# A third turn of lead for an image's parts, built at image 33 instead of 11, with another sharing-out of the weights' steps

## The chip, the core and the metric

The kernel runs on one NeuronCore of a Trainium2 chip. The metric is the device time of one execution in microseconds (us). The engines are named as in the profile: PE is TensorE, DVE is VectorE, ACT is ScalarE, POOL is GpSimd, SP is the queue that starts most DMAs.

## The reference

```python
# x: (160, 128, 32, 32) f32; U: 5 sets of 128*128*9 weights
s1 = (max(U) - min(U)) / 3;  v1 = s1 * floor(U / s1)
s2 = s1 / 5;                 v2 = s2 * floor((U - v1) / s2)
w = v1 + v2                       # the quantised weights of 5 grouped 3x3 convolutions
z = groupnorm(x, 32 groups of 4 channels, eps=1e-5)
out = x + conv3x3(z, w)           # images 0..31 by the first set, 32..63 by the second, ...
```

The sets are spread over the batch as channel groups; in the kernel's own order, set n serves the 32 images from 32n on. Each image is 128 channels (partitions) of 1024 values.

## The kernel before, in words

The whole program is one stream of 160 images on one core, written out in Python with a fixed order on each engine. In the loop of `run`, one pass is the **turn** of image `i`. In it, PE first does `sums_of_pairs(i + 1)` and then the main matmuls of image `i` (`conv`, `main`). The other engines work for images ahead of `i` and for the one behind.

Every image is split into a high and a low fp16 part, so that fp16 matmuls give the precision of fp32. There are two ways of doing an image:

- A **combined** image adds and subtracts neighbouring columns before the split. DVE and POOL make `v` (`combine`, L690 and L697 on DVE; `outer_columns` L678 and the subtraction at L708 on POOL), ACT makes the high part `vh` (L738), and DVE the low part `vl` (L744). Its PE work is 24 matmuls.
- An **uncombined** image has `z` (L714 on POOL, or L640 on ACT for the first of a group), `hi` (L648 on ACT), and on DVE `lo` (L751) and its row combinations (L764, L772, L773). Its PE work is 30 matmuls.

Up to image 29 the odd images from 7 on are combined; from 30 to 129 those with `i % 5` of 0, 2 or 4; later three in four.

The steps of an image `k` come in this order on DVE, in different turns:

1. `combine(k)`, if `k` is combined, at the end of the turn that `step_of(i, 4)` gives it;
2. after ACT's high part in the next turn (`step_of(i, 3)`), `vl` or `lo` with its combinations in the turn after that (`step_of(i, 2)`);
3. in turn `k - 1`, `pairs(k)`: two DVE instructions (L903, L905), which put halves of the sums that PE left in PSUM into the two banks in which `main(k)` accumulates. PE's `main(k)` waits for them; they wait for `sums_of_pairs(k)` on PE and for the copy `leave(k)` on ACT (L891).

The distance from these steps to the image's own turn is set by `step_of`:

```python
change = self.FURTHER + 4 - ahead
return [k for k in range(i + ahead + (i > change), i + ahead + 1 + (i >= change)) if k < self.imgs]
```

Until the turn `change` the step is for image `i + ahead`, after it for `i + ahead + 1`, and in that turn for both. With FURTHER = 11, two images are combined in turn 11, get their high parts in turn 12 and their low parts in turn 13. From then on low parts are ready three turns before their `main` instead of two. `consumed` uses the same constant: it tells from which turn on a chunk of two input images may be overwritten by a new load on SP.

DVE also measures eight early images itself (`BY_VECTOR`: 8, 10, 11, 14, 19, 24, 29, 34; L231 to L235); ACT measures the others. Further small DVE work belongs to the statistics of a group of images (L296 to L302, L307, L310), and POOL takes the power of the variance (L286).

While set n is in use, set n+1 is quantised. The weights' work is a list of DVE steps (L142 to L146, L162, L549, then L573 to L575), with two steps per column for ACT between them. The object `later` hands them out: each turn adds `pace` to what is due (36 / 22 for the first such set, 36 / 25 for the others), and `later.take(1)` issues one step if one is due and the next one isn't ACT's. There are up to three places in a turn: after L751 of an uncombined image, after the low part, and after `combine`.

The instruction `before` decides when POOL begins its share (L286, L678, L708, L714) for the image four turns ahead: these instructions wait for it, so that they run beside `pairs`[...].

```python
last = later.take(1, last)
if last:
    before = self.last_but_one(last)
```

Of the kernel before, what the change touches and what calls it, by code (L numbers as in the profile page):

```python
# [36 lines left out]
class Later:  # L37
# [25 lines left out]
    def finish(self):  # L63
        run(self.steps)
# [110 lines left out]
def last_of(steps, last=None):  # L175
    for last in steps:
        pass
    return last


def run(steps):

    while True:
        try:
            next(steps)
        except StopIteration as end:
            return end.value
# [134 lines left out]
def general_path(tc, keep, steps, x, u, out):  # L322
# [8 lines left out]
    with tc.If(far > 0), ExitStack() as ctx:  # L331
# [9 lines left out]
        for n in range(N_SETS):  # L341
            un = one.tile([P, C, TAPS], F32, tag="u", name=f"g_u{n}")
            nc.sync.dma_start(un, uv[n])
            wn = one.tile([P, C, TAPS], F32, tag="w", name=f"g_w{n}")
            k1, k2 = run(steps.quantise(one, un, f"g{n}", F32))
            nc.vector.tensor_scalar_mul(wn, k1, steps.s1)
            nc.vector.scalar_tensor_tensor(wn, k2, steps.s2, wn, ALU.mult, ALU.add)
# [38 lines left out]
class Main:  # L386
# [22 lines left out]


    STAT_LEAD = 15
    FURTHER = 11
    LOAD_LEAD = 18
    CHUNKS = 11
    STEADY = 7
# [557 lines left out]
    def step_of(self, i, ahead):  # L973


        change = self.FURTHER + 4 - ahead
        return [k for k in range(i + ahead + (i > change), i + ahead + 1 + (i >= change)) if k < self.imgs]

    def consumed(self, c):

        return max(i + 2 if self.by_hand(i) else i - 2 - (i > self.FURTHER + 6) for i in range(c * NB, c * NB + NB))

    def run(self):
# [54 lines left out]
        def measure(stage, *images):  # L1038
            for i in images:
                self.measure(i, (stage,))  # L1040
# [73 lines left out]
        later, turned = Later(), []  # L1114
        for i in range(self.imgs):
            n, b = self.place(i)


            def on_the_way(col):
                if col == self.COLS[1]:  # L1120
                    for st in ready:
                        st.means(self.pg)
                    for *column, parts in self.columns:
                        self.turn_column(*column, parts)
                        turned.append(column)
                    self.columns.clear()
                if col == self.COLS[2]:
                    for st in middle:
                        st.variances()

            if i < self.FIRST:
                if i == self.FIRST - 1:
                    self.sums_of_pairs(self.FIRST)

                j = (i - 1) % self.FIRST
                self.direct_hi(j, self.COLS[2])
                self.direct_lo(j, self.COLS[2])
                if i == 0:
                    self.stats[2].variances()
                    self.stats[2].deviation()  # L1140
                    self.stats[2].power()
                    self.stats[2].scales()
                    run(self.sums_across(0, nc.gpsimd))
                for col in self.COLS:
                    on_the_way(col)
            else:
                j = i - 1
                self.conv(i, on_the_way)
            ahead = i + min(10 + i // 3, self.STAT_LEAD + 1)
            to_measure = range(measured, min(self.imgs, ahead))  # L1150
            measured += len(to_measure)
            if i == 2:
                self.load_set(1)
            if b == self.per_set - 8 and n + 2 < N_SETS:
                self.load_set(n + 2)
            if n + 1 < N_SETS:
                if b == (4 if n == 0 else 1):
                    later = Later(
                        (s for col in self.COLS for s in self.make_column(n + 1, col, "later")),
                        36 / (self.per_set - 6 - b),  # L1160
                    )
            later.next_image()
            by_scalar = [k for k in to_measure if not self.by_vector(k)]
            by_vector = [k for k in to_measure if self.by_vector(k)]

            if i < self.FIRST:

                if i == 0:
                    measure(0, 8, 9, 10)
                if i == 1:  # L1170
                    self.normalise(4)
                    self.high_part(4)
                if i == 2:
                    self.leave(3)
                    self.normalise(5)
                    measure(1, 9)
                    self.high_part(5)
                    self.pairs(3)
                    self.low_part(4)
                    run(self.combinations(4))  # L1180
                    measure(0, 11)
                self.residual(j)
            else:

                last = None
                for k in self.step_of(i, 2):
                    if self.combined(k):
                        last = last_of(self.low_combined(k), last)
                    else:
                        self.low_part(k)  # L1190
                        later.take(1)
                        last = last_of(self.combinations(k), last)
                last = later.take(1, last)
                if last:
                    before = self.last_but_one(last)
                    for st in scaled:
                        self.after(st.power(), before)
                    for k in self.step_of(i, 4):
                        self.beside_pairs(k, before)
                if i > self.FIRST and self.by_hand(j):  # L1200
                    self.residual(j)
                for k in by_scalar:
                    self.measure(k, (0,))
                if i > self.FIRST and not self.by_hand(j):
                    self.residual(j)
                    self.accumulate(j)
                if i + 1 < self.imgs:
                    self.leave(i + 1)
                for st in ready:
                    if not st.late:  # L1210
                        st.deviations()
                for k in self.step_of(i, 3):
                    if self.combined(k):
                        self.high_combined(k)
                        continue
                    if self.by_scalar_too(k):
                        self.normalise(k)
                    self.high_part(k)
                for k in by_scalar:
                    self.measure(k, (1,))  # L1220
            for st in middle:
                st.deviation()
                if not st.late:
                    st.power()
                    st.scales()
            if i < self.FIRST:
                for st in ready:
                    st.deviations()
            for n_of, col in turned:
                self.keep_taps(n_of, col)  # L1230
                if col == self.COLS[-1]:
                    later = Later(self.sums_of_set(n_of), 3.0)
            turned = []

            if i >= self.FIRST:

                if i + 1 < self.imgs:
                    self.pairs(i + 1)
                for st in scaled:
                    st.scales_by_vector()  # L1240
                for k in self.step_of(i, 4):
                    if self.combined(k):
                        self.combine(k)
                    later.take(1)
                later.take_scalar()
                if b in (self.per_set - 4, self.per_set - 2):
                    later.finish()
                for st in ready:
                    if st.late:
                        st.deviations_by_vector()  # L1250
            scaled, middle, ready = [st for st in middle if st.late], ready, []
            if i >= self.FIRST:
                measure(0, *by_vector)
            for k in to_measure:
                group = self.group_of[k]
                if k + 1 == self.groups[group].stop:
                    ready.append(self.stats[group])
            while loaded * NB < self.imgs and (
                loaded * NB < i + self.LOAD_LEAD if loaded < self.CHUNKS
                else i >= self.consumed(loaded - self.CHUNKS)  # L1260
            ):
                self.load(loaded)
                due.append((i + 4, loaded))
                loaded += 1
            if due and due[0][0] <= i:
                self.store_input(due.pop(0)[1])
# [49 lines left out]
```

## Time and profile before

| | us |
|---|---|
| median of 3 runs (lowest, highest) | 966.23 (966.21, 966.47) |
| the profiled execution's own time | 964.56 |
| its span in the profile | 962.5 |
| PE busy | 927.8 (96%) |
| DVE busy | 902.6 (94%) |
| ACT busy | 862.7 (90%) |
| POOL busy | 460.1 (48%) |

The span runs from the first to the last instruction of the program; the execution has some 2 us around it. The profiled execution is 1.7 us under the median of the runs. Line numbers (L744) are those of the kernel's source, and the page gives for each group of instructions the busy time, the mean length of one in ns, and the idle time before it with what ended it. The ends of matmuls are modelled, so PE's busy share can't be read as a share of its peak; the starts of matmuls are recorded, and their distances tell more.

### The profile page before, as it was taken

The numbers are of one execution on the slowest core, as the hardware profiler recorded it, in microseconds if no ns is written. First come the engines' busy times: TensorE is split into PE (matmuls) and PEld (weight loads), VectorE is DVE, ScalarE is ACT, GpSimd is POOL, SyncE is SP. The second block draws the span as 40 slices with busy tenths as digits, with TensorE's granted clock in tenths as the row PEclk, the third lists the DMA queues.
The fourth block names the chain that finished last, engine by engine and source line by source line (L and its number), as shares of the span: only waits on it lengthen the run. The fifth ranks groups of instructions, "written<-read, shape, count | busy, mean of one in ns | idle before, by whom it ended". The sixth has DMA issues, their size and how long they took to land.

```text
span 962.5 us, 13034 instructions
## 1 busy us (share of the span) xinstructions
PE 927.8 (96%) x4432; PEld 433.8 (45%) x4432; DVE 902.6 (94%) x1269; ACT 862.7 (90%) x1167; POOL 460.1 (48%) x477
## 2 busy tenths in 40 slices
PE   2899989999999999999999999999999999999997
PEld 1344434444444444444444444444444444444443
DVE  7989999999899999989999999899999998999993
ACT  5879989999899999999999999999999999997660
POOL 4344434456445445554545445545444366565640
PEclk9999999999999999999999999999999999999999
DMA  9079999999999999999999999999999999856563
GB/s 349 36 267 345 334 348 320 325 321 325 328 321 323 317 295 308 272 306 254 295 251 289 284 293 297 282 277 286 267 273 267 282 279 269 172 91 107 91 107 112
DMA packets 67450, 254.22 MB, mean 264 GB/s; under 512 B 5296, under 2 KB 5296, under 8 KB 67376
## 3 DMA queue, kind: packets, MB, share of 16 engines
q1 hardware_dynamic: 45344, 173.09, 48.0%
q0 software_dynamic: 22032, 80.23, 44.4%
q8 instruction: 36, 0.59, 0.2%
q14 instruction: 38, 0.31, 0.1%
HBM read 89.19 MB, written 164.10 MB: 263 GB/s over the span
## 4 chain that ended last, share of the span: by engine, by line


## 5 line engine op out<-in xcount | busy, mean ns | idle before, releaser
L788 PE MATMUL eo<-hi,wt 128*128 128x496 f16 (+3 forms) x1170 | 310.8, 376 | 2.4 <-DVE eo L905 1.7
L843 PEld LDWEIGHTS <-wt 128*128 128x128 f16 x1884 | 183.9, 99 | 211.5 <-DVE eo L905 2.7
L744 DVE SCALAR_TENSOR_TENSOR vl<-v,rstd,vh 128x2048 f16<-128x2048 f32 x94 | 221.8, 2360 | 0.2 <-ACT vh L738 0.2
L843 PE MATMUL eo<-vh,wt 128*128 128x512 f16 x561 | 210.1, 375 | 1.2 <-DVE eo L905 1.2
L843 PE MATMUL eo<-vl,wt 128*128 128x512 f16 x561 | 210.1, 374 | 0.0
L738 ACT ACTIVATE vh<-v,rstd 128x2048 f16<-128x2048 f32 x94 | 188.2, 2002 | 4.8 <-DVE v L697 4.3
L929 ACT COPY sum<-eo 128x1024 f32<-128x1024 f32 x153 | 161.0, 1052 | 32.3 <-PE eo L843 31.7
L788 PEld LDWEIGHTS <-wt 128*128 128x128 f16 x1242 | 121.2, 99 | 142.8 <-DVE eo L905 4.9
L678 POOL TENSOR_SCALAR v<-xt,ngm 128x64 f32<-128x64 f32 x94 | 79.1, 842 | 202.0 <-DVE vl L744 86.9
L248 ACT ACTIVATE junk<-xt,mv 128x1024 uint8<-128x1024 f32 x152 | 174.4, 1148 | 0.3
L241 ACT ACTIVATE junk<-xt 128x1024 uint8<-128x1024 f32 x152 | 160.5, 1056 | 13.3 <-DMA xt<-in_x_dram 10.0
L714 POOL TENSOR_SCALAR z<-xt,ngm,rstd 128x1024 f32<-128x1024 f32 x49 | 93.3, 1904 | 165.1 <-DVE rows L773 55.0
L843 PEld LDWEIGHTS <-across 128*128 128x128 f16 x1128 | 110.8, 98 | 131.9 <-issue 4.9
L843 PE MATMUL eo<-rows,wt 128*128 128x512 f16 x378 | 143.5, 380 | 0.0
L953 POOL DMA_DIRECT2D out_dram<-sum x153 | 133.7, 874 | 14.4 <-ACT sum L929 6.6
L690 DVE TENSOR_TENSOR v<-xt 128x960 f32<-128x960 f32 x94 | 114.0, 1212 | 0.0
L843 PE MATMUL m<-vl,across 128*128 128x496 f16 (+1 forms) x282 | 106.4, 377 | 2.1 <-DVE vl L744 2.1
L891 ACT ACTIVATE m<-m 128x512 f32<-128x512 f32 x157 | 93.7, 597 | 14.1 <-PE m L843 13.7
L843 PE MATMUL m<-vh,across 128*128 128x496 f16 (+1 forms) x282 | 106.2, 376 | 0.2 <-ACT m L891 0.2
L708 POOL TENSOR_TENSOR v<-xt 128x512 f32<-128x512 f32 x94 | 97.2, 1034 | 0.0
L751 DVE TENSOR_TENSOR lo<-z,hi 128x1024 f16<-128x1024 f32 x66 | 80.6, 1221 | 0.0
L286 POOL TENSOR_TENSOR rstd<-ve,mhalf 128x8 f32<-128x8 f32 (+2 forms) x24 | 42.3, 1761 | 65.1 <-DVE rows L773 21.1
(150 smaller groups left out, 1166.3 us busy)
## 6 DMA issues: line engine op xcount, KB each, us to landing
xt<-in_x_dram SPq DMA_DIRECT2D x78, 1024.0 KB, 9.6
out_dram<-sum POOLq DMA_DIRECT2D x153, 512.0 KB, 8.7
out_dram<-xt SPq DMA_DIRECT2D x76, 1024.0 KB, 14.2
out_dram<-xt SPq DMA_DIRECT2D x7, 512.0 KB, 3.3
u<-in_L_conv_U_dram SPq DMA_DIRECT2D x4, 576.0 KB, 13.6
xt<-in_x_dram SPq DMA_DIRECT2D x4, 512.0 KB, 10.1
range<-in_L_conv_U_dram SPq DMA_DIRECT2D x3, 576.0 KB, 8.3
u<-in_L_conv_U_dram SPq DMA_DIRECT2D x2, 288.0 KB, 3.1
```

The lines of the kernel that those rows point to most:

```text
L241: self.nc.scalar.activation(junk, image, ACTF.Copy, scale=-1.0 / image.shape[1], accum_out=self.mv[:, j, 0:1],)
L248: self.nc.scalar.activation(junk, image, ACTF.Square, bias=self.mv[:, j, 0:1], accum_out=self.mv[:, j, 1:2],)
L690: nc.vector.tensor_tensor(self.view(v, 1, (511, 2), (half, H), (1, half - 1)), self.view(x, 1, (1, 2), (W, H), (2, half - 1)), self.view(x ...
L708: ins = nc.gpsimd.tensor_sub(self.v[i][:, 1536:], odd, even)
L714: ins = nc.gpsimd.tensor_scalar(z, self.image(i), st.ngm[:, j], st.rstd[:, j], ALU.add, ALU.mult)
L738: self.nc.scalar.mul(vh, self.v[i], st.rstd[:, j])
L744: yield self.nc.vector.scalar_tensor_tensor(vl, self.v[i], st.rstd[:, j], self.hi[i], ALU.mult, ALU.subtract)
L788: nc.tensor.matmul(self.bank(target, a)[:, first:end, c0:c1], self.wts[n, col][:, k, :], tile[:, s0 : s0 + 2 * (end - first) - 1 : 2, c0 + ...
L843: self.nc.tensor.matmul(out, weights, moving, start=start and j == 0, stop=False, skip_group_check=True)
L891: self.nc.scalar.mul(m2, self.m2_ps, 0.5)
L929: nc.scalar.copy(self.as_banks(i, self.sum[i]), self.flat(i, eo))
L953: added = self.nc.gpsimd.dma_start(self.ov[n, :, b], self.sum.pop(i), accum_op=ALU.add)
```

## The change

The constant that sets the change of lead goes from 11 to 33. The two images that are done in one turn are then 37 and 38, combined in turn 33, with high parts in turn 34 and low parts in turn 35. The place for a weights' step after the low part is closed in turns where image `i + 3` is combined. In such turns POOL's share waits for the last DVE instruction itself, and no longer for the one ahead of it.

```diff
-    FURTHER = 11
+    FURTHER = 33
...
-                last = later.take(1, last)
+                last = later.take(0 if self.combined(i + 3) else 1, last)
                 if last:
-                    before = self.last_but_one(last)
+                    before = last.ins if self.combined(i + 3) else self.last_but_one(last)
```

From turn 36 on, image `i + 3` is the one whose low part the turn makes. Up to turn 34 that is image `i + 2`. No instruction is added or taken out: each engine has the same instructions in another order.

## The prediction

> **What bounds the kernel.** I began with the page's busy times and went from there to the busy time by stage.
>
> ```profile
> PE 927.8 (96%) x4432; PEld 433.8 (45%) x4432; DVE 902.6 (94%) x1269; ACT 862.7 (90%) x1167; POOL 460.1 (48%) x477
> ```
>
> ```profile
> 100.00:125.00 25.00, 25.00 (x126) 12.10 (x124) 24.79 (x39) 24.87 (x35) 10.50 (x12) 1.00 1.04 332
> 125.00:150.00 25.00, 22.04 (x97) 9.49 (x95) 24.66 (x42) 21.40 (x30) 6.38 (x8) 0.93 1.04 341
> 150.00:175.00 25.00, 24.02 (x119) 11.35 (x118) 24.73 (x37) 24.49 (x36) 14.82 (x20) 1.00 1.04 321
> 225.00:250.00 25.00, 25.00 (x121) 11.69 (x119) 23.85 (x32) 24.70 (x34) 13.12 (x12) 1.00 1.05 310
> ```
>
> Columns: stretch, length, busy PE, PEld, DVE, ACT, POOL, then PE's clock, DMA share, GB/s. PE is full nearly everywhere, so time can be won only from its holes. The large hole lies at 125 to 150 us, where DVE is full too and the clock is 0.93. PE's timeline there:
>
> ```profile
> 126.86 0.37 PE L843 MATMUL eo<-vl,wt 128*128 128x496 f16 x1
> 127.43 0.38 PE L843 MATMUL m<-vh,across 128*128 128x512 f16 x1 [0.19 <-ACT m L891]
> 129.88 0.59 PE L843 MATMUL m<-vl,across 128*128 128x512 f16 x1 [2.08 <-DVE vl L744]
> 130.26 0.62 PE L843 MATMUL m<-vh,across 128*128 128x496 f16 x1
> 130.67 0.62 PE L843 MATMUL m<-vl,across 128*128 128x496 f16 x1
> ...
> 134.63 0.59 PE L788 MATMUL eo<-hi,wt 128*128 128x512 f16 x2 [0.70 <-DVE eo L905]
> ```
>
> Matmuls normally start 0.21 us apart. From 126.86 to 134.63 there are 13, worth 2.75 us, in 7.77 us: **5.02 us lost**. First PE waits for the low part of image 15; then it runs at half pace (starts 0.41 apart); then it waits for `pairs(14)`. This is turn 13, in which DVE makes two low parts. Read the same way, the other holes from image 11 on are 1.14 us at 157.4, 0.44 at 268.1, 0.64 at 494.8, 0.66 at 721.6 and 0.16 at 772.4, all at `pairs`. Sum 8.06 us; no version can win more here. The 0.94 us at 65.9 lies ahead of the first changed turn.
>
> The third view is DVE's timeline. I call what DVE runs from one `pairs` to the next the list of the later image. These are lists 36 and 37:
>
> ```profile
> 253.10 0.70 DVE L903 SCALAR_TENSOR_TENSOR eo<-m1b,m 128x512 f32<-128x512 f32 x1 [2.20 <-PE m1b L843]
> ...
> 254.44 1.15 DVE L690 TENSOR_TENSOR v<-xt 128x960 f32<-128x960 f32 x1
> ...
> 256.17 0.61 DVE L143 SCALAR_TENSOR_TENSOR tt<-nnn,s1nlo,tt 128x384 f32<-128x384 int16 x1
> 256.70 1.22 DVE L751 TENSOR_TENSOR lo<-z,hi 128x1024 f16<-128x1024 f32 x1
> 257.83 0.61 DVE L144 SCALAR_TENSOR_TENSOR tt<-tt,s1r,nnn 128x384 f32<-128x384 f32 x1
> 258.36 0.69 DVE L764 TENSOR_TENSOR rows<-lo 128x1024 f16<-128x1024 f16 x1
> ...
> 259.64 0.55 DVE L145 TENSOR_TENSOR lt<-tt,nnn 128x384 f16<-128x384 f32 x1
> 260.11 0.69 DVE L903 SCALAR_TENSOR_TENSOR eo<-m1a,m 128x512 f32<-128x512 f32 x1
> ...
> 262.12 1.99 DVE L690 TENSOR_TENSOR v<-xt 128x960 f32<-128x960 f32 x1
> 264.03 0.74 DVE L697 SCALAR_TENSOR_TENSOR v<-xt,twice 128x512 f32<-128x512 f32 x1
> 264.69 2.34 DVE L744 SCALAR_TENSOR_TENSOR vl<-v,rstd,vh 128x2048 f16<-128x2048 f32 x1
> 266.96 0.34 DVE L146 TENSOR_TENSOR k<-nnn,lt 128x384 f16<-128x384 int16 x1
> ```
>
> Start to next start is what an instruction costs DVE: `pairs` P 1.33, `combine` C 1.73, `vl` V 2.26, an uncombined low part U 2.41 (1.13 + 1.28), steps 143 and 144 0.53 each, 145 0.47, 146 0.27. Elsewhere: 142 0.65, 162 0.66, 549 0.47, a measurement 1.68, a group's deviations 0.54. L307 with its waits costs about 0.4 where nothing blocks it. PE's turns, by starts: a combined image's sums 2.54 and main 2.54, an uncombined one's 1.29 and 5.10, so 11.47 us for two.
>
> [...]L744 is 2.34 long and its successor starts after 2.27. [...]L690 at 262.12 takes 1.99 instead of 1.15 while POOL's L708 runs from 262.06 for 1.03. [...]
>
> **The change, part by part.** Instructions and queues stay; the order moves. The changed listing gives every list. I lay it out with the slots above, on the clock of before.
>
> *Removed at 11 to 13.* List 14 was P, C, deviations, measurement, V, U and two steps (ended 133.15). It is now P, deviations, measurement, V, 142 = 6.46. Start: list 11 loses a step (0.47), so `pairs(11)` starts at 109.53; list 12 (4.33) is then held by ACT's `leave(12)` at 114.00. In list 13, `lo(14)` ended 7.40 after `pairs(12)`; one step for another (0.65 to 0.47) makes 7.22, so `pairs(13)` starts at 121.15. V(15) is ready at 121.15 + 1.33 + 0.54 + 1.68 + 2.34 = 127.04 and PE wants it at 127.07: **stall 0.1**.
>
> *Two turns of lead at images 14 to 34.* List 15 (6.53) is in time by 0.5. List 16 has L307 right after POOL's power, with POOL's `z` next; in before such an L307 was locked out to 1.08 long. At 1.2 V(17) comes 1.0 late: **stall 1.0** (0.2 unlocked, 1.2 at worst). List 17, with a measurement, is 7.81: U(18) **0.4** late. Lists 18 to 28 are in time by 0.36 or more. Sum 1.5 (0.7 to 2.5), against 5.02 + 1.14 = 6.16. Gain **4.7**. ACT makes one high part fewer in turn 12, which only helps `leave(14)` (127.38 in before).
>
> *Added at 33 to 35.* DVE has room there: the trace shows `pairs(30)`, 33 and 35 waiting for PE or ACT. PE sets the start of `pairs(35)`, 253.10 in both. List 36 is now P, C, 143, V, U, 144, 145 = 9.26, so `pairs(36)` ends at 253.10 + 9.26 + 1.43 = 263.79; PE wanted it at 261.87: **stall 2.0**. V(37) itself is ready at 259.03 for 259.33. ACT has 37's high part, 1.9, more in turn 34, so `leave(36)` may be 2 late (259.7); that falls under the same stall. List 37 keeps its lock (6.85 measured without 146), so `main(37)` waits 0.5. Together 2.5 against 0.44: cost **2.0**.
>
> *The weights' steps.* Up to image 34 the test looks at the other kind of image, and no turn takes over two steps. Later the uncombined turns take three and some lists grow: 51 by 1.66 against 1.31 of slack (0.4 late), 61 by 1.7 against 1.23 (0.45), 62 0.15, 96 by 1.92 against 1.61 (0.35). Sum 1.35. The holes at 494.8, 721.6 and 772.4 (1.46) fall away, since lists 77, 117 and 126 lose 1.0 to 1.5 of steps. Net **0** (−1 to +1). The later `before`: where no step followed V, POOL's first instruction was locked out until V's end anyway; L286 before list 61 does start later, which is in its 1.7. Behind a waiting L678 or L286 on POOL stand L708, L714 and the DMA starts of L953; C waits for L678, ACT's high part for L714. I take 0 otherwise; without that cover it costs POOL up to 2.3 a turn, on an engine 48% busy, and C up to 0.9 where P is too short to hide it.
>
> *SP and the rest.* Loads for chunks 20 to 30 may be issued a turn later (5.7 us). The tightest, image 44's, landed at 206.2 and was first read at 220.2; with PE 4.7 earlier some 3.6 us stay. So 0, at worst 2. POOL's DMA starts keep their places; PE's order is the same.
>
> Sum: −4.7 + 2.0 + 0 = **−2.7 us**: own time 964.56 to 961.9, span 959.8; from the median 966.23, 963.6, rounded to 963.7 for the loads.
>
> **Rivals.** *Hidden:* list 36 costs nothing because DVE's idle time before it absorbs it; then 4.7 is won: 961.5. Idle in lists 34 and 35 speaks for it; against it, `pairs(35)` can't move ahead of PE. Chance 0.12. *Clock:* the 2.0 us stall halves PE's clock for 3 us as at 130. That costs 1.6, of which 0.9 shows, as list 37 binds: 964.5 to 965. Gaps of 1.1 us left the clock alone, 2.6 did not. Chance 0.22. *Two turns are too few:* lists 15 to 28 add up to 81.0 us against PE's 7 × 11.47 = 80.3, so anything above the slots becomes a stall. [...] it turns slower than before from 0.19 a list. Against it: the 117 lists of before in which DVE was late exceed their slots by 9.2 us in all, 0.08 each, mostly at L307. Chance 0.13. That the steps don't move as said is visible up to image 34 and priced.
>
> **Numbers.** The main case (0.53) has 962.4 to 964.9. A measurement here can tell 0.2%, 1.9 us, from no change, so faster means under 964.3. Main gives 0.47 of faster and Hidden 0.12; Clock and the rest of Main give 0.27 of same; slower is 0.14, the last case and 0.01 of Clock. Range 961.4 to 966.6: outside lie half of Hidden and the slow case.
>
> **What would show it.** Right: no half pace near 130; PE gaps of about 1 near 138 and 2 us just ahead of `main(36)`; no gap at lists 77 and 117. Wrong: over 4 us of gaps in images 14 to 30, no gap at 36, or waits of ACT for loads near 220 us.

## The result, and the profile after

The changed kernel takes **981.06 us** (median of 6 runs, 979.68 to 982.02), the kernel before 966.35 beside it: ratio 1.0151, 95% interval 1.0137 to 1.0165. It is **14.7 us slower**; a gain of 2.7 us was forecast. (One of the six executions of the kernel before took 1655 us; without it their median is 966.23.) The profiled execution has a span of 979.0 us and an own time of 980.82, against 962.5 and 964.56 before.

The busy times, first row of the page of the changed kernel:

```profile
PE 930.2 (95%) x4432; PEld 433.0 (44%) x4432; DVE 908.8 (93%) x1269; ACT 862.9 (88%) x1167; POOL 389.0 (40%) x477
```

No engine has noticeably more to do (DVE 6 us), POOL has 71 us less. So the 16.5 us by which the span grew are waiting. The busy times by stage, with the same columns as in the prediction, first of the changed kernel:

```profile
125.00:150.00 25.00, 23.10 (x110) 10.46 (x109) 24.66 (x41) 23.33 (x34) 8.79 (x10) 1.00 1.04 331
...
225.00:250.00 25.00, 21.71 (x96) 9.53 (x95) 19.27 (x25) 19.93 (x29) 11.34 (x13) 0.93 1.04 329
...
400.00:425.00 25.00, 19.95 (x95) 8.85 (x94) 23.73 (x34) 21.36 (x29) 10.49 (x12) 0.98 1.03 326
590.00:615.00 25.00, 22.19 (x106) 10.00 (x105) 23.63 (x36) 22.48 (x31) 9.04 (x10) 1.00 1.05 323
```

Then the last two of them in the kernel before:

```profile
400.00:425.00 25.00, 25.00 (x119) 11.51 (x118) 22.20 (x30) 23.53 (x32) 15.95 (x13) 1.00 1.02 288
590.00:615.00 25.00, 25.00 (x121) 11.68 (x119) 22.81 (x30) 24.70 (x34) 14.55 (x12) 1.00 1.03 298
```

PE has filled up in 125 to 150 us (22.04 before, now 23.10, at full clock). But three stretches that were full of PE before, 225 to 250, 400 to 425 and 590 to 615, now have holes of 3 to 5 us each. They lie one set of weights apart: 32 images are about 184 us. The view of waits says what ended them. These are PE's rows of it, with the total in us, how often, and the longest:

```profile
PE m L843 <- DVE across L574: 6.4, 2, 3.3
PE small L558 <- DVE m L549: 3.3, 3, 1.4
PE eo L788 <- DVE eo L905: 2.8, 3, 1.8
...
PE m L843 <- DVE wt L574: 2.4, 2, 1.4
```

Three of these four are waits for weights, and none of the three is in the profile of before: PE waits for the sums of the next set (`across` and `wt`, L573 to L575) and for the last DVE step of a column (`m`, L549), which PE transposes at L558. The first of the long ones, on PE's timeline:

```profile
229.39 0.37 PE L843 MATMUL eo<-vh,wt 128*128 128x496 f16 x1
229.60 0.37 PE L843 MATMUL eo<-vl,wt 128*128 128x496 f16 x1
233.26 0.61 PE L843 MATMUL m<-vh,across 128*128 128x512 f16 x1 [3.29 <-DVE across L574]
233.66 0.63 PE L843 MATMUL m<-vl,across 128*128 128x512 f16 x1
...
236.53 0.37 PE L843 MATMUL m1a<-vh,across 128*128 128x496 f16 x1
```

And what DVE did meanwhile:

```profile
229.46 0.70 DVE L905 SCALAR_TENSOR_TENSOR eo<-m1b,m 128x512 f32<-128x512 f32 x1
230.07 1.15 DVE L690 TENSOR_TENSOR v<-xt 128x960 f32<-128x960 f32 x1
231.13 0.75 DVE L697 SCALAR_TENSOR_TENSOR v<-xt,twice 128x512 f32<-128x512 f32 x1
231.79 0.35 DVE L574 TENSOR_TENSOR wt<-wt 128x384 f16<-128x384 f16 x1
232.18 0.36 DVE L575 TENSOR_TENSOR wt<-wt 128x384 f16<-128x384 f16 x1
232.46 0.35 DVE L573 TENSOR_TENSOR across<-wt 128x384 f16<-128x384 f16 x1
232.84 0.36 DVE L574 TENSOR_TENSOR across<-across,wt 128x384 f16<-128x384 f16 x1
233.24 0.36 DVE L575 TENSOR_TENSOR across<-across,wt 128x384 f16<-128x384 f16 x1
```

Image 32 is the first of set 1. PE has ended main(30) and turns to `sums_of_pairs(32)`, for which it needs `across`. DVE makes the sums only now, behind `pairs` and `combine`, in list 32; in the kernel before the same instructions stand in lists 29 and 30. There the last two of them ran some 9 us before PE first needed `across`, at 231.03:

```profile
220.93 0.35 DVE L574 TENSOR_TENSOR across<-across,wt 128x384 f16<-128x384 f16 x1
221.32 0.36 DVE L575 TENSOR_TENSOR across<-across,wt 128x384 f16<-128x384 f16 x1
```

In the changed kernel PE stands for 3.45 us beyond its usual distance, and then its starts are 0.4 us apart, half pace (granted clock 0.50), until 236.5, another 1.5 us. Image 64 loses 3.30 + 1.55 us in the same way at 421.3. Images 96 and 128 are uncombined and need only `wt`: 1.6 us at 610.0, 1.14 at 793.0. The transposes come late at 120.0 (0.90), at 412.4 and at 599.8:

```profile
412.44 0.38 PE L843 MATMUL eo<-rows,wt 128*128 128x496 f16 x1
414.12 0.35 PE L558 MATMUL small<-ident,m 128*128 128x128 f16 x3 [1.30 <-DVE m L549]
```

Sum: 5.0 + 4.85 + 1.6 + 1.14 + 0.90 + 1.47 + 1.54 = **16.5 us for weights that are late**.

Why they are late is told by the order on DVE. From list 39 to 61 the changed kernel's lists hold 1, 0, 3, 1, 1 weights' steps in every five, that is 6, where the pace makes 7.2 due (36 / 25 a turn). In the kernel before, lists 35 to 59 hold all 36 steps, 7.2 in every five. The steps that find no place pile up, until `later.finish()`, in two late turns of a set, issues what is left: in list 62 the end of the third column, in list 64 all six of the sums. The third column's L549 moves from list 59 to 62, 91 to 94 and 123 to 126, and the last sums from 30, 62, 94 and 126 to 32, 64, 96 and 128, the list of the very image that needs them first.

### The profile page after: what moved, and what is told of

It is laid out like the page before. It is cut to its first block, busy times and chain, and to the rows that moved or that the text cites. A ratio compares the mean times of both kernels' runs of the same rounds, so it can differ in the third digit from the quotient of the medians.

```text
span 979.0 us, 13017 instructions
## 1 busy us (share of the span) xinstructions
PE 930.2 (95%) x4432; PEld 433.0 (44%) x4432; DVE 908.8 (93%) x1269; ACT 862.9 (88%) x1167; POOL 389.0 (40%) x477
## 4 chain that ended last, share of the span: by engine, by line
## 5 line engine op out<-in xcount | busy, mean ns | idle before, releaser
L744 DVE SCALAR_TENSOR_TENSOR vl<-v,rstd,vh 128x2048 f16<-128x2048 f32 x94 | 220.3, 2343 | 0.7 <-ACT vh L738 0.7
L678 POOL TENSOR_SCALAR v<-xt,ngm 128x64 f32<-128x64 f32 x94 | 40.9, 436 | 266.1 <-DVE vl L744 135.6
L714 POOL TENSOR_SCALAR z<-xt,ngm,rstd 128x1024 f32<-128x1024 f32 x49 | 60.8, 1240 | 182.9 <-DVE vl L744 84.9
L690 DVE TENSOR_TENSOR v<-xt 128x960 f32<-128x960 f32 x94 | 117.7, 1253 | 0.0
L903 DVE SCALAR_TENSOR_TENSOR eo<-m1b,m 128x512 f32<-128x512 f32 x79 | 54.7, 693 | 19.6 <-PE m1b L843 10.0
```

Source lines behind the costliest of these rows:

```text
L690: nc.vector.tensor_tensor(self.view(v, 1, (511, 2), (half, H), (1, half - 1)), self.view(x, 1, (1, 2), (W, H), (2, half - 1)), self.view(x ...
L744: yield self.nc.vector.scalar_tensor_tensor(vl, self.v[i], st.rstd[:, j], self.hi[i], ALU.mult, ALU.subtract)
```

## The experiments

The theory after the result: the closed places make the weights' steps late, and that alone makes the kernel slower. Rivals: the third turn of lead at 33 costs more than was thought; POOL's later start delays the images; the order of the steps inside the lists, and not their time, does it. The kernel before ran beside each: 966.41 us with the first four kernels below, 966.75 with the next four, 966.33 with those after them, and 967.33 with one that says so. "Lost" below is the time by which the distance from one start of a matmul to the next exceeds the usual one (0.21 us), in the profiled execution.

### The lead alone

```diff
-    FURTHER = 11
+    FURTHER = 33
```

> Only the constant: the two-image turns at 33 to 35, the weights' steps shared out as before. Theory A (deadline): the slowdown comes from the weights' steps, which end so late that PE waits for the weights of the next set at images 32, 64, 96 and 128. Then this run has no such waits, since its last sums stand in the DVE lists of images 30, 62, 94 and 126 as in the kernel before; what is left is the gap of 2.0 us at main(36), 0.4 at main(37) and some waits at images 9 to 19: 965 to 968 us. Theory B (lead): the two-turn lead for images 14 to 34 is what costs; then 974 to 981 us.

Measured: 965.13 us, ratio 0.9987 (0.9981 to 0.9994). No wait for weights. Lost at main(36) 1.64 and at main(37) 0.72. The lead is worth a gain of 1.3 us and is not what makes the changed kernel slower.

### The steps alone

```diff
-                last = later.take(1, last)
+                last = later.take(0 if self.combined(i + 3) else 1, last)
                 if last:
-                    before = self.last_but_one(last)
+                    before = last.ins if self.combined(i + 3) else self.last_but_one(last)
```

> Only the two lines on the weights' steps, with the constant at 11. The sums of set 1 stand in list 30 here, those of sets 2, 3 and 4 in lists 64, 96 and 128 as in the changed kernel. Theory A (deadline): PE waits near images 64 (some 4.9 us with the slow clock, 1.5 for the transposes), 96 (1.6 and 1.5) and 128 (1.1), together 10.7, less some 1.5 of holes that go: about 975 us (973 to 978). Theory B (lead): about 966 us.

Measured: 977.09 us, ratio 1.0109 (1.0094 to 1.0124), 10.7 us slower. Waits at images 64, 96 and 128, as in the changed kernel. The one at image 32 is missing: with the lead at 11, the image that the test looks at is from turn 14 on the one whose low part is made, and the sums of set 1 stand at list 30, in time. In the changed kernel it is another image up to turn 34, and the sums stand at list 32. So the two halves of the change do not add up: −1.3 + 10.7 is 9.4, and the 5.0 us at image 32 come from both together.

### The lead and POOL's later start

```diff
-    FURTHER = 11
+    FURTHER = 33
...
-                    before = self.last_but_one(last)
+                    before = last.ins if self.combined(i + 3) else self.last_but_one(last)
```

> The constant at 33 and POOL's later start (it waits for the last DVE instruction where image i + 3 is combined), but the place for a step after the low part stays open. The sums stand in lists 30, 62, 94, 126. Theory A (deadline): within 1 us of the run with the constant alone. Theory C (POOL's start): the later start makes combine and L307 wait; then 5 us or more slower than the constant alone.

Measured: 965.68 us, ratio 0.9991 (0.9984 to 0.9997), which overlaps with that of the lead alone. POOL's later start costs nothing that shows. What it does is seen in POOL's groups (busy time and mean ns, then idle before), first with the lead alone, then in this run:

```profile
L678 POOL TENSOR_SCALAR v<-xt,ngm 128x64 f32<-128x64 f32 x94 | 81.2, 864 | 212.0 <-DVE vl L744 95.1 <-issue 55.7 <-DVE rows L772 37.2
L678 POOL TENSOR_SCALAR v<-xt,ngm 128x64 f32<-128x64 f32 x94 | 43.7, 465 | 248.3 <-DVE vl L744 92.3 <-issue 84.6 <-DVE rows L772 28.1
```

L714 goes from 1858 to 1244 ns in the same way. A part of the longer times was standing behind DVE. The kernel before (L678 842 ns) shows it: 74 of its 94 instructions of L678 start while a DVE instruction other than those of `pairs` runs; 73 of these end 0.24 to 0.30 us after it, whenever they started, and take 0.38 to 2.34 us. The other 20, beside `pairs` or an idle DVE, take 0.37 to 0.38 us. In the changed kernel (436 ns), with POOL's later start, 31 start inside such a DVE instruction and 63 do not. POOL's busy time falls from 462 to 390 us, DVE's rises from 903 to 908, and the kernel's time stays.

### The rest of the steps issued two turns earlier

The changed kernel with

```diff
-                if b in (self.per_set - 4, self.per_set - 2):
+                if b in (self.per_set - 6, self.per_set - 4):
```

> The changed kernel with one number changed: the remaining steps of a set are all issued in turns 26 and 28 of a set instead of 28 and 30, so that the sums stand in lists 30, 62, 94 and 126. Theory A (deadline): the waits of PE for the sums and the slow clock after them (5.0, 4.9, 1.6 and 1.1 us in the changed kernel) go, the waits for the transposes stay or grow, and the bunched steps cost 1 to 3 us: 968 to 973 us. Theories B and C: within 2 us of the changed kernel's 981.

Measured: 973.19 us, ratio 1.0065 (1.0050 to 1.0081). The waits for sums are gone, and with them about half of the loss (6.8 us of 14.7 are left). But list 60 now holds six steps in one bunch and is late, and other bunches follow. PE's timeline at main(61), one list after that bunch, and then at the transposes of a later set:

```profile
405.05 0.37 PE L843 MATMUL m1a<-vl,across 128*128 128x496 f16 x1
407.99 1.43 PE L788 MATMUL eo<-hi,wt 128*128 128x512 f16 x3 [2.57 <-DVE eo L905]
409.21 0.63 PE L843 MATMUL eo<-rows,wt 128*128 128x512 f16 x1
...
580.70 0.38 PE L843 MATMUL eo<-rows,wt 128*128 128x496 f16 x1
584.00 0.35 PE L558 MATMUL small<-ident,m 128*128 128x128 f16 x3 [2.92 <-DVE m L549]
584.18 0.80 PE L788 MATMUL eo<-hi,wt 128*128 128x496 f16 x3
```

A bunch issued earlier removes the wait for the sums but makes others.

### The places closed only in the first half of a set

The changed kernel with

```diff
-                last = later.take(0 if self.combined(i + 3) else 1, last)
+                last = later.take(0 if self.combined(i + 3) and b < 16 else 1, last)
```

> The changed kernel, but the place after the low part is closed only in the first 16 turns of a set; after that there are as many places as before. The last sums stand in lists 30, 62, 94, 126 without any bunching. Theory A (deadline): all waits for sums and transposes from image 30 on go, some 15 us; what is left is as with the constant alone: 965 to 968 us. Rivals (lead, POOL's later start, longer uncombined lists): 970 or more.

Measured: 967.36 us, ratio 1.0006 (0.9997 to 1.0014). `before` and the order of the first half stay as in the changed kernel; only the steps of the second half catch up, and the sums stand at lists 30, 62, 94 and 126 again. The stretches of 225 and 400 us of this kernel:

```profile
225.00:250.00 25.00, 25.00 (x121) 11.69 (x119) 22.72 (x32) 23.93 (x34) 12.38 (x13) 1.00 1.04 317
...
400.00:425.00 25.00, 25.00 (x119) 11.48 (x118) 23.21 (x31) 23.77 (x31) 10.71 (x13) 1.00 1.02 291
```

PE is full there as before, and all but 0.6 of the 14.7 us are won back. Against the lead alone (0.9987) this run is still 1.9 us slower; its profile has holes of 1.45, 0.65 and 1.23 us at 374, 545 and 722 us, which are waits for `pairs` and not for weights. So the closed places have another cost, but a small one; the bulk is lost by lateness at the end of a set.

### The kernel before, with a slower pace

```diff
-                        36 / (self.per_set - 6 - b),
+                        36 / (self.per_set - b),
```

> The kernel before with one number changed: the pace at which the weights' steps fall due is 36 over 28 (first set) and 31 images instead of 22 and 25. The last sums stand in lists 32, 64, 96, 128, as in the changed kernel; lead, places and POOL's start are those of before. Theory A (deadline): the lateness alone costs it: waits of about 5, 5, 1.6 and 1.1 us for the sums and up to 1.5 at each set for the transposes, less about 1 of other holes: 974 to 980 us. Rivals: within 2 us of before.

Measured: 981.31 us, ratio 1.0152 (1.0138 to 1.0166), as slow as the changed kernel with neither half of the change in it. Only the steps come later. Its PE at image 32:

```profile
229.43 0.37 PE L843 MATMUL eo<-vl,wt 128*128 128x496 f16 x1
235.75 0.61 PE L843 MATMUL m<-vh,across 128*128 128x512 f16 x1 [5.95 <-DVE across L574]
236.15 0.63 PE L843 MATMUL m<-vl,across 128*128 128x512 f16 x1
```

With the run before it, this settles the cause from both sides: take the lateness out of the changed kernel and the loss goes; put it into the kernel before and a like loss appears, with waits for the same things. That the totals agree within 0.3 us is luck in part: here PE waits 5.95 us at image 32, against 3.29 in the changed kernel, and less for the sums of images 96 and 128.

### The lead at 31, and a slower pace of the first set with it

What is left is where the extra low part should stand. With

```diff
-    FURTHER = 11
+    FURTHER = 31
```

> The constant at 31 and the steps shared out as before: the two low parts fall into DVE's list 34, which has no other low part or step, instead of list 36, which has three steps. Theory (the gap at main(36) is DVE's long list): in the kernel with 33 main(34) had over 5 us in hand, so the second low part (2.3) and combine (1.7) fit, and the gaps of 1.6 to 2.0 at main(36) and some 0.3 of 0.7 at main(37) go: about 963 us, 2 under the run with 33 alone (965.1). Rival: the gap is due to the move itself, wherever it stands; then 965 again, with the gap near main(34).

Measured: 964.63 us, ratio 0.9978 (0.9969 to 0.9988). Its median is 2.1 us under the kernel before, where the lead at 33 had 1.3, but the two intervals overlap. 1.07 us are still lost at main(36) and 0.72 at main(37). Then, with the pace of the first set 36 / 24 instead of 36 / 22 as well:

> The constant at 31, and the first set's pace 36 over 24 images instead of 22, the other sets as before. Its last sums still stand in list 30. Theory: the stalls at images 14 to 19 come from DVE lists that are too full for a lead of two turns; two steps fewer up to list 19 (about 1 us) take 1 us off them: 962 us, 1 under the kernel with 31 alone. Rival: those stalls have another cause (ACT or loads): no change from 31 alone.

Measured: 964.31 us, ratio 0.9978 (0.9971 to 0.9985). No difference from the lead at 31 alone shows: slowing the first set's pace wins nothing here.

### The later sets begun two turns later

```diff
-    FURTHER = 11
+    FURTHER = 31
...
-                if b == (4 if n == 0 else 1):
+                if b == (4 if n == 0 else 3):
```

The pace of the later sets is counted from this turn and becomes 36 / 23 with it.

> The kernel before with the two images done in one turn at image 31, and with the later sets of weights begun two turns later in their set, so that the list of main(36), which holds the one extra low part, has no weights' step. The sums of the sets still stand at lists 61 to 62, 94 and 126, in time. Theory (a step in list 36 is what keeps main(36) waiting about 1.1 us and main(37) 0.7 us in the run with the lead at 31): both gaps shrink to under 0.5, about 963 us, 1 us below that run. Rival (DVE is full over the whole stretch from 31 to 37, so that a step taken out of one list only moves the wait to the next): the gaps are the same in sum, 964.5 us.

Measured: **962.59 us**, ratio 0.9956 (0.9943 to 0.9970), the lowest of all, from five executions. (The expectation misplaces one thing: the two low parts stand in list 34, and their lateness is carried on to list 36.) DVE's list 36, up to `pairs(36)`, in this kernel:

```profile
252.05 0.69 DVE L903 SCALAR_TENSOR_TENSOR eo<-m1b,m 128x512 f32<-128x512 f32 x1
...
255.11 1.22 DVE L751 TENSOR_TENSOR lo<-z,hi 128x1024 f16<-128x1024 f32 x1
256.36 0.69 DVE L764 TENSOR_TENSOR rows<-lo 128x1024 f16<-128x1024 f16 x1
...
257.64 0.69 DVE L903 SCALAR_TENSOR_TENSOR eo<-m1a,m 128x512 f32<-128x512 f32 x1
```

There are no steps in it: 5.59 us from one `pairs` to the next. With the lead at 31 alone it has three and takes 7.00, and `pairs(36)` starts at 260.50. PE then goes from the sums of image 37 to main(36) without a hole (starts at 259.91 and 260.12), and nothing is lost at main(37) either. From 240 to 290 us no other hole appears, so the rival, that a wait would only move, falls there.

Does the later start pay by itself? The kernel before with that line alone:

> The kernel before, with its lead at 11, and only the later sets of weights begun two turns later in their set (and with a pace of 36 / 23 instead of 36 / 25, so that they end in the same turn as before). Theory (the later start pays where a step stands beside the one extra low part of a lead at 31, and only there): the hole of 0.44 us at pairs(37) goes, and the holes near 495, 722 and 772 us, 1.46 together, give way to about 1.5 us elsewhere, as in the run with both; 966.0 us, within 0.1% of before. Rival (the later start pays by itself wherever the lead is): it takes off the 2.0 us that it took off the run with the lead at 31, 964.3 us.

Measured: 965.90 us against 967.33, ratio 0.9987 (0.9980 to 0.9994), 1.3 us faster. Theory said 0.4, rival 2.0, and the interval (0.6 to 1.9) excludes both. The profile shows the theory's parts, the hole at pairs(37) gone and 1.3 us of others at 687 and 723 us in the place of three; where the remaining 0.9 us come from stays open, for ahead of 180 us this execution has 1.9 us more of holes than that of before, with the same order of instructions there. The ratios of the lead at 31 alone (0.9978) and of the later start alone (0.9987) multiply to 0.9965, which lies inside the interval of the run with both. So the times do not show that the two help each other; that the hole at main(36) goes is seen in the profile.

### The lead at 29

```diff
-    FURTHER = 11
+    FURTHER = 29
```

> The kernel before with the two images done in one turn at image 29; the list with two low parts is then 32, ahead of the stretch of images 33 to 37 in which DVE makes more. Theory (where DVE has room decides, and the room lies ahead of list 33): a gap at main(32) of at most 1 us and none at 36, 964 us. Rival (lists 30 to 33 have no room either, since the set's own statistics and steps stand there): over 2 us of gaps at 32 and 33, 965.5 us.

Measured: 964.40 us, ratio 0.9980 (0.9973 to 0.9987); with the later start of the sets as well:

> Both at once: the two images in one turn at image 29, and the later sets of weights begun two turns later. Theory (the gaps after image 31 come from the steps of the next set beside an extra low part): none over 0.5 us between images 31 and 38, 963 us. Rival (the extra low part costs its own length of DVE wherever it stands): 1 to 2 us of gaps, 964.5 to 965 us.

Measured: 963.92 us, ratio 0.9974 (0.9965 to 0.9983). Both lose 0.8 us at 229.5, where the sums of image 32 wait for `vl(32)`, and 0.6 at 239, ahead of main(32). That is 1.4 us in each, more than the theory of either run allowed; the rival of the second run, 1 to 2 us of gaps, fits. The second `combine` stands in list 31, ahead of `vl(32)`, with L690 1.98 us long at 225.40, and the second low part in list 32. None is left at 36. So list 34 has room for a second low part, as long as the steps stay out of the lists behind it, and lists 31 and 32 have less. By the times alone the leads at 29 and 31 can't be told apart.

## Why the prediction was wrong

**The step that failed is "The weights' steps … Net 0 (−1 to +1)".** It read from the changed listing how many steps each DVE list has, priced longer and shorter lists by the time that each DVE instruction takes, against the slack of `pairs`, and stopped there. It never asked by when PE needs what the steps make. The same listing showed L549 and L575 in other lists: three later for the transposes, two later for the sums. Measured on the two profiled executions, that term is +16.4 us net: 16.5 of late weights, and the rest of the stretches from 280 us on at about zero (the holes at lists 77, 117 and 126 went as forecast, others of 0.5 to 0.8 us came). Lead alone, steps alone, places back late and slow pace agree on it. None of the rivals had this mechanism; *Two turns are too few* expected a slower kernel, but for another reason.

The other steps, by the two profiled executions:

| step | forecast, us | measured, us | by |
|---|---|---|---|
| removed at 11–13, two turns of lead after | −4.7 | −2.7 | lost from 110 to 180 us: 6.76 before, 4.96 after, of which 0.90 is the transposes |
| added at 33–35 | +2.0 | +2.1 | lost from 250 to 280 us: 0.55 before, 2.63 after |
| weights' steps | 0 | +16.4 | above |
| ahead of 110 us | 0 | +0.85 | 13.28 before, 14.13 after |
| sum | −2.7 | +16.6 | spans 979.0 − 962.5 = 16.5 |

**Removed at 11 to 13: mechanism right, size off.** The half pace near 130 is gone, as said:

```profile
128.47 0.38 PE L843 MATMUL m<-vh,across 128*128 128x512 f16 x1
129.25 0.38 PE L843 MATMUL m<-vl,across 128*128 128x512 f16 x1 [0.40 <-DVE vl L744]
129.47 0.37 PE L843 MATMUL m<-vh,across 128*128 128x496 f16 x1
```

The stalls that replace it are 0.56 here (0.1 forecast), 1.05 at 140.5 ("about 1 near 138"), 0.79 at 149.0 (0.4), and 1.02 at 164.4, a wait of a group's statistics (L273) that the prediction did not look at. Together they are 3.4 us where 1.5 were forecast: this is the mis-sized term.

The 0.56 come from the start of `pairs(11)`: 111.7 instead of the 109.53 derived for it. ACT had waited 2.56 us for the load of image 12 at 62.0, and PE lost 1.85 us at 90.2, waiting for `leave`. That is not the change: the kernel before with only the later start of the sets waits 1.28 us for this load and loses 1.29 at the same place, and four traces without such a wait of ACT (before, lead and POOL's start, places back late, slow pace) have no hole at 90. Traces differ in when the load lands, and the profiled one of before was 1.7 us under its median. Places back late has the changed kernel's lists up to 18 and no such wait: there `pairs(11)` starts at 109.28 and main(15) does not wait. (Two slips in that sum change little: 114.00 + 7.22 is 121.22 and not 121.15, and PE's first use of `vl(15)` comes one matmul, 0.21 us, after 127.07.) But 1.02, 0.80 and 1.46 us at 138.1, 146.6 and 162.0 remain, and from 110 to 180 us it loses only 2.9 us less than before. So the load explains the first stall and not the rest.

The wait at 164.4 is what the prediction calls a lock and priced elsewhere, an instruction of POOL or DVE that takes longer beside one of the other: POOL's first step of these statistics (L267, from 162.50) takes 2.20 us beside DVE's L744 (2.34 us from 162.29), against 0.64 in the kernel before. Two executions with equal holes at 90 us (1.29), the later start alone and the lead at 31 with later sets, lose 21.9 and 18.5 us up to 180 us; by them the lead is worth 3.4 us there.

**Added at 33 to 35: right.** DVE's list 36 and what PE lost to it:

```profile
256.90 0.70 DVE L903 SCALAR_TENSOR_TENSOR eo<-m1b,m 128x512 f32<-128x512 f32 x1 [0.25 <-PE m1b L843]
...
260.50 2.35 DVE L744 SCALAR_TENSOR_TENSOR vl<-v,rstd,vh 128x2048 f16<-128x2048 f32 x1
262.76 1.22 DVE L751 TENSOR_TENSOR lo<-z,hi 128x1024 f16<-128x1024 f32 x1
...
266.17 0.69 DVE L903 SCALAR_TENSOR_TENSOR eo<-m1a,m 128x512 f32<-128x512 f32 x1
```

```profile
265.46 0.37 PE L843 MATMUL m1b<-vl,across 128*128 128x496 f16 x1
267.65 0.81 PE L788 MATMUL eo<-hi,wt 128*128 128x512 f16 x3 [1.81 <-DVE eo L905]
```

The list is 9.27 us long (9.26 forecast), starts when PE releases it, and costs 1.98 us (2.0); main(37) loses 0.44 (0.5).

**POOL and SP: right.** POOL's later start is nil within 0.6 us, and no wait of ACT for loads appears near 220 us.

**The rivals.** *Hidden* fell: the stall at 36 came in full. *Clock* fell where it was put: after 1.98 us at main(36) the next three matmuls, from 267.65 to the start of the fourth at 268.29, take 0.64 us, full speed, and the granted clock is 1.00 from 267.18 to 270.60. Half pace came instead at images 32 and 64, where nobody had looked. *Two turns are too few* fell: the stalls of images 14 to 30 are the 3.4 us above, under the 4 named as its sign.

## What to carry over

Background work that is handed out in spare places has a deadline as well as a length. When an edit closes places, count what falls due against the places left in one period (here 7.2 against 6 in five turns), find the instruction that first reads the result, and compare its time with where the last step then stands; a listing of the new order shows both. And a bunch that a "finish" call issues is not a safety net when it stands in the list of the image that needs it.

## What was unexpected of the hardware

How long PE stands does not alone tell whether its clock halves. After 1.98 us at 265.5 it kept full speed; after 2.24 us at 127.4 (before the change) and 2.73 us at 405.05 (with the steps two turns earlier) it ran at half pace for 3.2 to 3.3 us; but after 3.09 us at 580.7, in the same kernel as the 2.73, the three matmuls at 584.18 took 0.64 us, full speed. In the changed kernel the granted clock is halved from 233.05 to 236.46 and from 424.19 to 427.61, 3.41 us each, and the two starts are 56 times 3.413 us apart. In the kernel before it is halved for 3.41 us from 40.94 and from 129.68, starts that are 26 times 3.413 us apart. Here are three stretches of that length in the kernel with the steps two turns earlier (their bounds are an estimate, worked out from this spacing; PE's busy time is the first number after the length, its clock the third from the end):

```profile
404.49:407.90 3.41, 0.93 (x5) 0.22 (x3) 3.38 (x9) 3.38 (x5) 1.40 (x3) 1.00 1.05 368
407.91:411.30 3.39, 3.31 (x8) 1.18 (x9) 3.32 (x8) 3.17 (x5) 0.78 (x1) 0.50 1.03 309
581.99:585.39 3.40, 1.39 (x9) 0.78 (x10) 3.30 (x5) 2.77 (x5) 0.00 (x0) 1.00 1.03 348
```

The hole of 2.73 us lay almost wholly in the first of them, in which PE was busy for 0.93 us, and the second ran at half rate. The hole of 3.09 us reached into the third from the stretch ahead of it; the third still had 1.39 us of work, and the clock stayed. The hole at 265.5 is divided in the same way, by the same spacing, at 267.18: PE was busy for 2.06 of the 3.41 us before this bound and for 2.95 of the 3.42 us after it, both at a clock of 1.00. How little work goes with a halved clock is not shown: 1.34 us stood ahead of half rate in the kernel before (126.27 to 129.68), 1.39 here did not, and with the steps alone PE had 1.72 us of work from 126 to 130, and the clock is 0.50 from 130 to 134. So a hole of 2 to 3.5 us cost some 1.5 us more (at images 32 and 64) or nothing (at main(36)). That it depends on where a hole lies in this spacing is the author's estimate from these few cases. The prediction had read its one hole of this size by its length alone.

POOL's start relative to DVE changed POOL's durations without changing the time. Between the lead alone and the lead with POOL's later start, L678 went from 864 to 465 ns and 72 us of POOL's busy time disappeared, and the two medians, 965.13 and 965.68 us, are within 0.1%. POOL's busy time before was in part standing behind DVE (73 of 94 instructions of L678, above), and so overstated its work.
